# A hand-written engine order, single products between block steps, and most edge lists built inside the first batch

## The chip, the cores and the metric

The kernel runs on one core of a Trainium2 chip. The metric is the device time of one execution in microseconds (us). The kernel before takes 2917.2 us, the median of 3 runs (2911.98 to 2935.88).

## What is computed

A graph attention layer over 16 batches of 1024 nodes with 512 features and 8 heads of 64, all in float32, then a residual sum and a layer norm without weights.

```python
q = (x @ Wq + bq).reshape(b, n, H, HD)
k = (x @ Wk + bk).reshape(b, n, H, HD)
v = (x @ Wv + bv).reshape(b, n, H, HD)
scores = jnp.einsum('bqhd,bkhd->bhqk', q, k) / jnp.sqrt(jnp.float32(HD))
scores = scores + (1.0 - adj)[None, None, :, :] * -1000000000.0
attn = jax.nn.softmax(scores, axis=-1)
out = jnp.einsum('bhqk,bkhd->bqhd', attn, v).reshape(b, n, d)
return out @ Wo + bo
...
x = _layernorm(x + _L0_gnn_ref(x, adj, ...), axis=-1)
```

The adjacency matrix is the same for all 16 batches. It is sparse and uneven: entry (i, j) is 1 with a probability that falls as one over the square root of i times j, so the first rows have many neighbours and the last ones few.

## The kernel before

Scores are worked out only where the adjacency is 1. The nodes are cut into 8 tiles of 128 queries. `edges(t)` turns the rows of tile `t` into a list of edges: `MAX8` rounds find the key numbers (10 rounds for tile 0, two for each of the others), small matrix products spread them so that one edge stands on one partition, and the results are `key_row` and `query_row` (which rows to fetch) and `sums` (a 128 by 128 matrix of zeros and ones for each block, which adds the edges of a query). A block is 128 edges. `BLOCKS = (11, 6, 4, 4, 3, 3, 3, 3)` gives the blocks of each tile, 37 for one batch and 592 in all.

**The front of a batch.** For each of its 8 tiles of x: four transposes on TensorE (`transpose_x`), and three projections of four products each (`project`, 128x512 outputs): q and k leave PSUM by VectorE, v by ScalarE. q goes to the DRAM array `q_rows`, k and v to `kv_rows`, both held twice, for even and odd batches. `norm` squares q and k on ScalarE and reduces the squares on VectorE, for a guard at the end. After the last tile one small product gives the mean of v (`pm`), which is row 1024 of `kv_rows`; the gathers of a batch need that row.

**A block `n`.** GpSimd issues two indirect DMAs (`gather`): `kvg` fetches 128 rows of 1024 numbers, `qg` 128 rows of 512. `scores` multiplies q and k and reduces over each head on VectorE, then ScalarE takes the exponential; `weigh` multiplies v with it on VectorE (two instructions of 256 columns); `add_up` adds the edges on TensorE into the tile's `sum` (two products of 264 and 256 columns). After a tile's last block, `normalise` divides (VectorE) and `transpose_o` turns the result (TensorE, out by ScalarE).

**Finishing a tile.** `finish` makes the output projection `po` (four products), adds x, takes the statistics on VectorE, raises to the power -0.5 on GpSimd, scales on VectorE, and stores.

Buffers around the change: 8 `kvg` (also used by `edges`), 8 `qg`, 4 `y`, 6 `oT`, 4 PSUM banks with the tag `fill` for everything but `sum`, and 2 x 2 banks for `sum`.

**What sets the order.** The program is written as a loop over blocks: in step `n` it gathers block n + 6, scores n + 2, weighs n + 1, adds up n, and then does one piece of the next batch's front (a whole projection of four products) or, when none is left, one whole `finish`. All 8 `edges` come ahead of that loop, each followed by one tile of the front of batch 0. But this is not the order in which the engines run it: a scheduler in the framework takes the program as a priority list and reorders each engine's instructions by its own estimate of when each is ready. Within an engine the order is then fixed, and an instruction that waits holds up all behind it.

Of the kernel before, what the change touches and what calls it, by code (L numbers as in the profile page):

```python
# [24 lines left out]
KEYCODE = 2000.0  # L25
# [101 lines left out]
def kernel(  # L127
# [57 lines left out]
    with ExitStack() as main:  # L185
# [16 lines left out]
        code = one.tile([P, N], F32, name="code")  # L202
        nc.gpsimd.iota(code, pattern=[[-1, N]], base=int(KEYCODE), channel_multiplier=0, allow_small_or_imprecise_dtypes=True)

        place = one.tile([P, max(BLOCKS) * P], F32, name="place")
        nc.gpsimd.iota(place, pattern=[[1, max(BLOCKS) * P]], base=0, channel_multiplier=0, allow_small_or_imprecise_dtypes=True)
        placed = one.tile([P, max(BLOCKS)], F32, name="placed")
        nc.gpsimd.iota(placed, pattern=[[P, max(BLOCKS)]], base=0, channel_multiplier=1, allow_small_or_imprecise_dtypes=True)
# [4 lines left out]
        nc.vector.tensor_scalar(before, place[:, 0:P], query[:, 0:1], None, op0=OP.is_gt)  # L213
# [27 lines left out]
        def bias_setup():  # L241
# [7 lines left out]
            bvb = work.tile([P, NPAIR, P], F32, tag="y", name="bvb", bufs=4)  # L249
# [7 lines left out]

        def edges(t):
            nb, J = BLOCKS[t], DEGREE[t]
            a = work.tile([P, N], F32, tag="kvg", name=f"a_{t}", bufs=8)  # L260
            nc.sync.dma_start(a, adj[ds(t * P, P), :])
            v = work.tile([P, N], F32, tag="kvg", name=f"codes_{t}", bufs=8)
            nc.gpsimd.tensor_tensor(v, a, code, op=OP.mult)
            st = small.tile([P, 4], F32, name="est")
            deg, end, lim, lone = (st[:, i:i + 1] for i in range(4))
            kl = small.tile([P, J + 2], F32, tag=f"kl{J}", name=f"kl_{t}", bufs=2)

            j = work.tile([P, N], F32, tag="kvg", name=f"j_{t}", bufs=8)
            nc.scalar.activation(j, a, AF.Copy, accum_out=deg)
# [9 lines left out]
            nc.vector.tensor_scalar(lone, kl[:, 0:1], 0.0, KEYCODE - N, op0=OP.is_le, op1=OP.mult)  # L279
            nc.vector.tensor_tensor(kl[:, 0:1], kl[:, 0:1], lone, op=OP.add)  # L280
            nc.vector.tensor_scalar(deg, deg, 1.0, None, op0=OP.max)
            po = fill_psum(f"poff_{t}")
            nc.tensor.matmul(po[:, 0:1], before, deg, start=True, stop=True)
            nc.vector.tensor_copy(kl[:, J:J + 1], po[:, 0:1])
# [5 lines left out]
            )  # L290

            ge = work.tile([P, max(BLOCKS) * P], F32, tag="ge", name=f"ge_{t}", bufs=1)
            of = work.tile([P, max(BLOCKS) * P], F32, tag="of", name=f"of_{t}", bufs=1)
# [4 lines left out]
            for i0 in range(0, nb, step):  # L298
# [4 lines left out]
                for i in range(n):  # L303
                    nc.tensor.matmul(g[:, i, :], of[:, ts(i0 + i, P)], kl, start=True, stop=True)
# [211 lines left out]
        for n in range(AHEAD):  # L516
            gather(n)
# [91 lines left out]
```

## Time and profile before

| | |
|---|---|
| median of 3 runs | 2917.2 us |
| profiled execution | 2934.78 us, span 2933.0 us |
| TensorE (PE) | busy 2578.4 us, 88%, at a mean granted clock of 0.951 |
| VectorE (DVE) | busy 2013.0 us, 69% |
| GpSimd (POOL) | busy 1488.4 us, 51% |
| ScalarE (ACT) | busy 488.1 us, 17% |
| DMA | 678.04 MB, 231 GB/s over the span |

The profile is of one execution. In it, L348 is line 348 of the kernel printed above; PEld is TensorE's weight load, which overlaps PE. Each float32 matrix product of 512 columns appears as two records, so that a projection of four products is "x8". In a timeline row the columns are the start, the duration (both us), the engine, the line, the operation, output<-input and the count; in brackets stands the idle time of that engine just before, and what ended it.

### The profile page before, as it was taken

What the parts mean: (1) busy time and instruction counts of PE and PEld (TensorE: products, weight loads), DVE (VectorE), ACT (ScalarE), POOL (GpSimd) and SP (SyncE); (2) the same over time, 40 slices, a digit from 0 to 9 for tenths busy, and PEclk for the clock granted to TensorE, in tenths of its full rate; (3) what the DMA queues carried; (4) which work ended last, traced back from release to release, by engine and by line L of the source; (5) the groups of instructions that cost most, each with busy time, mean ns of one, the idle gap of its engine ahead of it and who ended that gap; (6) DMA issues with size and microseconds to landing.
All of it is one profiled execution on the core that took longest, in us unless ns stands there. A gap on an engine that the chain in (4) does not pass through costs nothing.

```text
span 2933.0 us, 27152 instructions
## 1 busy us (share of the span) xinstructions
PE 2578.4 (88%) x7659; PEld 1377.0 (47%) x7659; DVE 2013.0 (69%) x4375; ACT 488.1 (17%) x1300; POOL 1488.4 (51%) x1462
## 2 busy tenths in 40 slices
PE   2889889998989989899889988989898989989977
PEld 1445444544445444444444444444444444445443
DVE  6657756767676676766667676666756767676687
ACT  2312111111111111111111111111111111111110
POOL 3035544636455464654546455464644636455474
PEclk8999999999999999999999999999999999999988
DMA  4258776767767676776777767677766767767685
GB/s 147 79 210 279 229 243 220 264 226 247 237 225 254 235 240 233 235 250 225 250 231 255 236 214 254 227 242 240 246 230 222 257 229 244 243 225 261 209 285 168
DMA packets 228682, 678.04 MB, mean 231 GB/s; under 512 B 29454, under 2 KB 29466, under 8 KB 228524
## 3 DMA queue, kind: packets, MB, share of 16 engines
q0 software_dynamic: 132608, 465.64, 48.8%
q1 hardware_dynamic: 93344, 205.60, 20.0%
q10 hardware_dynamic: 2572, 4.99, 0.5%
q8 instruction: 63, 1.03, 0.1%
q14 instruction: 95, 0.78, 0.1%
HBM read 541.86 MB, written 134.25 MB: 231 GB/s over the span
## 4 chain that ended last, share of the span: by engine, by line
DMA 27%; DVE 25%; issue 21%; POOL 15%; PE 12%; ACT 1%; POOLq 0%; DVEq 0%; SPq 0%; ACTq 0%
DMA kvg<-kv_rows,key_row 22%; POOL qg L451 8%; DVE s L460 5%; DVE pv L468 5%; DVE qg L458 4%; POOL kvg L446 4%; PE po L424 3%; POOL rstd L433 2%; DVE kv L370 2%; DVE nrm L356 2%; DVE stats L429 2%; PE pq L348 2%; PE pv L348 2%; DVE y L426 2%; PE pk L348 2%
## 5 line engine op out<-in xcount | busy, mean ns | idle before, releaser
L446 POOL DMA_INDIRECT kvg<-kv_rows,key_row x592 | 599.0, 1012 | 907.7 <-DVE pv L468 800.5
L458 DVE TENSOR_TENSOR qg<-qg,kvg 128x512 f32<-128x512 f32 x592 | 407.6, 693 | 545.3 <-DMA kvg<-kv_rows,key_row 540.7
L451 POOL DMA_INDIRECT qg<-q_rows,query_row x592 | 615.7, 1040 | 259.6 <-issue 105.7
L348 PE MATMUL pv<-wv,xT 128*128 128x512 f32 x1024 | 481.1, 614 | 42.8 <-DVE q L363 42.8
L424 PE MATMUL po<-wo,oT 128*128 128x512 f32 x1024 | 505.0, 639 | 2.8 <-ACT oT L504 2.0
L348 PE MATMUL pq<-wq,xT 128*128 128x512 f32 x1024 | 473.1, 605 | 34.9 <-ACT xT L341 34.9
L468 DVE TENSOR_TENSOR pv<-kvg,pv 128x256 f32<-128x256 f32 x1184 | 487.7, 436 | 0.0
L348 PE MATMUL pk<-wk,xT 128*128 128x512 f32 x1024 | 460.8, 593 | 2.0 <-DVE kv L370 2.0
L460 DVE TENSOR_REDUCE s<-qg 128x8 f32<-128x512 f32 x592 | 400.3, 676 | 0.0
L481 PE MATMUL sum<-pv,sums 128*128 128x264 f32 x1184 | 371.6, 396 | 13.8 <-DVE pv L468 9.9
L482 PE MATMUL sum<-pv,sums 128*128 128x256 f32 x1184 | 363.2, 389 | 4.7 <-DVE pv L468 4.4
L424 PEld LDWEIGHTS po<-wo,oT 128*128 128x128 f32 x1024 | 206.1, 208 | 252.5 <-issue 233.0
L348 PEld LDWEIGHTS pv<-wv,xT 128*128 128x128 f32 x1024 | 199.3, 197 | 255.1 <-issue 197.7
L481 PEld LDWEIGHTS sum<-pv,sums 128*128 128x128 f32 x1184 | 218.5, 195 | 202.1 <-issue 171.9
L348 PEld LDWEIGHTS pq<-wq,xT 128*128 128x128 f32 x1024 | 193.8, 193 | 241.4 <-issue 187.9
L348 PEld LDWEIGHTS pk<-wk,xT 128*128 128x128 f32 x1024 | 185.8, 190 | 187.3 <-issue 184.1
L482 PEld LDWEIGHTS sum<-pv,sums 128*128 128x128 f32 x1184 | 229.9, 195 | 49.0 <-DVE pv L468 8.0
L356 DVE TENSOR_REDUCE nrm<-sq 128x8 f32<-128x512 f32 x256 | 174.6, 682 | 77.5 <-ACT sq L355 77.5
L355 ACT ACTIVATE sq<-q 128x512 f32<-128x512 f32 x128 | 80.6, 630 | 876.3 <-DVE q L363 755.7
L463 ACT ACTIVATE pv<-s 128x8 f32<-128x8 f32 x592 | 118.4, 203 | 546.7 <-PE sum L482 266.4
L416 POOL TENSOR_TENSOR y<-y,bo_bc 128x512 f32<-128x512 f32 x128 | 166.1, 1304 | 60.1 <-DMA y<-in_x_dram 50.3
L434 DVE TENSOR_SCALAR y<-y,mv,rstd 128x512 f32<-128x512 f32 x128 | 73.9, 577 | 162.6 <-POOL rstd L433 162.6
(96 smaller groups left out, 1551.4 us busy)
## 6 DMA issues: line engine op xcount, KB each, us to landing
kv_rows<-kv SPq DMA_DIRECT2D x128, 512.0 KB
x<-in_x_dram SPq DMA_DIRECT2D x128, 256.0 KB
y<-in_x_dram SPq DMA_DIRECT2D x128, 256.0 KB
q_rows<-q SPq DMA_DIRECT2D x128, 256.0 KB
out_dram<-y SPq DMA_DIRECT2D x128, 256.0 KB
qg<-q_rows,query_row POOLq DMA_INDIRECT x592, 5.0
kvg<-kv_rows,key_row POOLq DMA_INDIRECT x592, 5.4
a<-in_adj_dram SPq DMA_DIRECT2D x8, 512.0 KB
```

What stands on the lines that cost most here:

```text
L348: nc.tensor.matmul(p, XT[b, t][:, ts(c, P)], W[name][:, c, :], start=(c == 0), stop=(c == NPAIR - 1))
L356: nc.vector.tensor_reduce(NRM[b][:, i, t, :], sq.rearrange("p (h d) -> p h d", d=HD), axis=AX.X, op=OP.add)
L416: nc.gpsimd.tensor_tensor(y, y, bo_bc, op=OP.add)
L424: nc.tensor.matmul(p, o[:, ts(c, P)], W["o"][:, c, :], start=(c == 0), stop=(c == NPAIR - 1))
L446: nc.gpsimd.indirect_dma_start(out=KG[n], out_offset=None, in_=kv_rows[b % 2], in_offset=bass.IndirectOffsetOnAxis(ap=key_row[:, g:g + 1], ...
L451: nc.gpsimd.indirect_dma_start(out=QG[n], out_offset=None, in_=q_rows[b % 2], in_offset=bass.IndirectOffsetOnAxis(ap=query_row[:, g:g + 1] ...
L458: nc.vector.tensor_tensor(m, m, KG[n][:, 0:D], op=OP.mult)
L460: nc.vector.tensor_reduce(s, m.rearrange("p (h d) -> p h d", d=HD), axis=AX.X, op=OP.add)
L463: nc.scalar.activation(PV[n][:, HD2:HD2 + HEADS], s, AF.Exp)
L468: nc.vector.tensor_tensor(pv[:, ds(i * (HD2 + HEADS), HD2)].rearrange("p (h d) -> p h d", d=HD), v[:, ds(D + i * HD2, HD2)].rearrange("p ( ...
L481: nc.tensor.matmul(SUM[b, t][:, 0, 0:HD2 + HEADS], m, pv[:, 0:HD2 + HEADS], **kw)
L482: nc.tensor.matmul(SUM[b, t][:, 1, 0:HD2], m, pv[:, HD2 + HEADS:], **kw)
```

## The change

1. The loop over blocks stands inside `tc.manual_schedule()`: each engine runs its instructions in the order in which the program writes them. What is written before the loop is still ordered by the scheduler.
2. In that loop an operation that needs a result of step `n` from another engine is put into a later step by `later(k, fn)`: a projection's exit from PSUM comes one step after its last product, the square one step later, the reduction one more; the output's statistics follow the same rule.
3. Projections are no longer whole pieces. `product` hands out single products with a cost (`PRODUCT = 0.86`, four transposes `TRANSPOSE = 0.44`), and each step spends a fixed `share` of a batch's total cost: `per_batch / 37`.
4. `edges` became a generator of five or six pieces. Tiles 0 and 1 are built before the loop, tiles 2 to 7 inside batch 0, one piece a step, from the steps in `EDGES_FROM`.
5. Gathers run 8 blocks ahead (6 before), q ahead of k and v. The gathers of a new batch are held until the step in which that batch's mean has been stored (`set_up`).
6. `weigh` is one instruction of 512 columns; the head sums stand at the end of `pv` and not in its middle, so the two adding products have 256 and 264 columns.
7. The scale of the layer norm goes from VectorE to ScalarE (`activation` with a bias and a scale per row); for the bias GpSimd makes two more operations of 128x1 per tile. The add of x and the bias waits two steps after its load. There are 7 `y`, 7 `oT`, 7 `qg`, 2 `q`, 4 `xT`, and `edges` has two buffers of its own.

```diff
+AHEAD = 8
+EDGES_FROM = (0, 0, 1, 5, 9, 12, 15, 18)
+PRODUCT = 0.86
+TRANSPOSE = 0.44
...
+        def later(k, fn):
+            if now[0] is None:
+                fn()
+            else:
+                plan.setdefault(now[0] + k, []).append(fn)
...
+        def product(name, lhs, w, out):
+
+            def unit(c):
+                if c == 0:
+                    PS[name] = fill_psum(name)
+                p = PS[name]
+                nc.tensor.matmul(p, lhs()[:, ts(c, P)], w[:, c, :], start=(c == 0), stop=(c == NPAIR - 1))
+                if c == NPAIR - 1:
+                    del PS[name]
+                    later(1, lambda: out(p))
+
+            return [(PRODUCT, lambda c=c: unit(c)) for c in range(NPAIR)]
...
+                def root():
+                    nc.gpsimd.tensor_tensor(rstd[:, 0:1], rstd[:, 0:1], neg_half, op=OP.pow)
+                    nc.gpsimd.tensor_tensor(rstd[:, 1:2], rstd[:, 0:1], mv[:, 0:1], op=OP.mult)
+                    nc.gpsimd.tensor_tensor(rstd[:, 1:2], rstd[:, 1:2], neg_one, op=OP.mult)
+
+                def norm_out():
+                    nc.scalar.activation(y, y, AF.Identity, bias=rstd[:, 1:2], scale=rstd[:, 0:1])
+                    nc.sync.dma_start(out_ap[b, ds(t * P, P), :], y)
+                    del Y[b, t]
+
+                later(1, root)
+                later(3, norm_out)
...
         def weigh(n):
             v, pv = KG.pop(n), PV[n]
-            for i in range(2):
-                nc.vector.tensor_tensor(
-                    pv[:, ds(i * (HD2 + HEADS), HD2)].rearrange("p (h d) -> p h d", d=HD),
...
+            nc.vector.tensor_tensor(
+                pv[:, 0:D].rearrange("p (h d) -> p h d", d=HD),
+                v[:, D:].rearrange("p (h d) -> p h d", d=HD),
+                pv[:, D:, None].to_broadcast([P, HEADS, HD]), op=OP.mult,
+            )
...
+        per_batch = NT * (4 * NPAIR * PRODUCT + 2 * TRANSPOSE)
+        share = per_batch / NB
+        prep = {EDGES_FROM[t]: edges(t) for t in range(2, NT)}
+        preps = []
+        with tc.manual_schedule():
...
+            while n < total or plan or done or finishing:
+                now[0] = n
+                if n < total and blocks[n][1:] == (0, 0):
+                    b = blocks[n][0]
+                    if b + 1 < B:
+                        fronts = [u for t in range(NT) for u in front(b + 1, t)]
+                while gathered < min(n + AHEAD + 1, total) and blocks[gathered][0] in set_up:
+                    gather(gathered)
+                    gathered += 1
+                if n + 1 < total:
+                    weigh(n + 1)
+                if n + 2 < total:
+                    scores(n + 2)
+                for fn in plan.pop(n, ()):
+                    fn()
+                if n + 2 < total:
+                    exponentials(n + 2)
+                if n < total:
+                    add_up(n)
+                for bb, tt in done[:2]:
+                    if (bb, tt) not in Y:
+                        load_y(bb, tt)
+                credit += share
+                while credit > 0:
+                    if not fronts and not finishing and done and n > loaded.get(done[0], n):
+                        finishing = finish(*done.pop(0))
+                    units = finishing or fronts
+                    if not units:
+                        break
+                    cost, fn = units.pop(0)
+                    fn()
+                    credit -= cost
+                credit = min(credit, share)
+                if n in prep:
+                    preps.append(prep.pop(n))
+                preps = [g for g in preps if next(g, True) is None]
+                n += 1
```

Three places show how the instructions move. In the names, `pv_83` is the weighed block 83, `qg` and `kvg` its gathered rows, and in `po_1_0` or `y_1_0` the numbers are batch and tile.

VectorE in batch 2 (blocks 74 to 110), before:

```order
L458 TENSOR_TENSOR qg_87_3194<-qg_87_3194,kvg_87_3192 128x512
L458 TENSOR_TENSOR qg_88_3218<-qg_88_3218,kvg_88_3216 128x512
L468 TENSOR_TENSOR pv_82_3177<-kvg_82_3062,pv_82_3177 128x256 x2
L460 TENSOR_REDUCE s_85_3253<-qg_85_3140 128x8
L458 TENSOR_TENSOR qg_89_3250<-qg_89_3250,kvg_89_3248 128x512
L363 SCALAR_TENSOR_TENSOR q_3_1_3132<-pq_3_1_3127,bq_bc_104 128x512
L458 TENSOR_TENSOR qg_90_3271<-qg_90_3271,kvg_90_3269 128x512
L356 TENSOR_REDUCE nrm_3_3023<-sq_3_1_0_3135 128x8
L468 TENSOR_TENSOR pv_83_3199<-kvg_83_3094,pv_83_3199 128x256 x2
```

and VectorE there now:

```order
L520 TENSOR_TENSOR pv_83_3126<-kvg_83_2958,pv_83_3126 128x512
L509 TENSOR_TENSOR qg_84_2983<-qg_84_2983,kvg_84_2985 128x512
L511 TENSOR_REDUCE s_84_3141<-qg_84_2983 128x8
L401 TENSOR_TENSOR kv_3_2_3145<-pk_3_2_3110,bk_bc_103 128x512
L520 TENSOR_TENSOR pv_84_3147<-kvg_84_2985,pv_84_3147 128x512
L509 TENSOR_TENSOR qg_85_3016<-qg_85_3016,kvg_85_3018 128x512
L511 TENSOR_REDUCE s_85_3160<-qg_85_3016 128x8
L386 TENSOR_REDUCE nrm_3_2996<-sq_3_2_0_3143 128x8
```

Before, the product with q and k of block 90 stands ahead of the weighing of block 83, so a block's `kvg` buffer is held over seven further blocks, and the exit of the projection `q_3_1` stands behind products that need the gathers of blocks 88 and 89. Now each block is weighed one step after its scores, and a step's exits follow its one weigh and its one score.

TensorE at the mean of batch 2 (`pm_2`), in batch 1, before:

```order
L348 MATMUL pv_2_7_2639<-wv_67,xT_2_7_2527 128x512 x4
L481 MATMUL sum_1_4_2674<-pv_62_2610,sums_110 128x264
L482 MATMUL sum_1_4_2674<-pv_62_2610,sums_110 128x256
L481 MATMUL sum_1_4_2674<-pv_63_2633,sums_110 128x264
L482 MATMUL sum_1_4_2674<-pv_63_2633,sums_110 128x256
L386 MATMUL pm_2_2647<-vsum_2_2141,mean_92 1x512
L424 MATMUL po_1_0_2677<-wo_69,oT_1_0_2295 128x512 x4
```

and TensorE there now:

```order
L374 MATMUL pv_2_7_2541<-wv_67,xT_2_7_2424 128x512 x3
L553 MATMUL poT_1_3_2578<-ident_58,o_1_3_2556 128x128 x4
L532 MATMUL sum_1_4_2563<-pv_63_2534,sums_108 128x256
L533 MATMUL sum_1_4_2563<-pv_63_2534,sums_108 128x264
L356 MATMUL pxT_3_1_2591<-ident_58,x_3_1_2322 128x128 x4
L374 MATMUL po_0_6_2596<-wo_69,oT_0_6_1881 128x512 x3
L532 MATMUL sum_1_4_2563<-pv_64_2561,sums_108 128x256
L533 MATMUL sum_1_4_2563<-pv_64_2561,sums_108 128x264
L374 MATMUL po_0_6_2596<-wo_69,oT_0_6_1881 128x512
L374 MATMUL po_0_7_2623<-wo_69,oT_0_7_1966 128x512 x3
L422 MATMUL pm_2_2635<-vsum_2_2093,mean_92 1x512
```

Before, only two blocks' additions stand between the last product of v and the product that needs the sum of v. Now seven products of the output projection, eight transposes and two blocks stand there, and the output products of a tile are split by the additions.

GpSimd at the same place, before:

```order
L446 DMA kvg_76_2899<-kv_rows_0_115,key_row_111 128x1024
L416 TENSOR_TENSOR y_1_4_2654<-y_1_4_2654,bo_bc_72 128x512
L451 DMA qg_79_2972<-q_rows_0_117,query_row_112 128x512
L446 DMA kvg_77_2915<-kv_rows_0_115,key_row_111 128x1024
L433 TENSOR_TENSOR rstd_2750<-rstd_2750,neg_half_88 128x1
L451 DMA qg_80_2988<-q_rows_0_117,query_row_112 128x512
```

and GpSimd there now:

```order
L495 DMA qg_74_2698<-q_rows_0_115,query_row_110 128x512
L500 DMA kvg_74_2700<-kv_rows_0_113,key_row_109 128x1024
L495 DMA qg_75_2702<-q_rows_0_115,query_row_110 128x512
L500 DMA kvg_75_2704<-kv_rows_0_113,key_row_109 128x1024
L455 TENSOR_TENSOR y_1_1_2655<-y_1_1_2655,bo_bc_72 128x512
L471 TENSOR_TENSOR rstd_2685<-rstd_2685,neg_half_88 128x1
L472 TENSOR_TENSOR rstd_2685<-rstd_2685,mv_2682 128x1
L473 TENSOR_TENSOR rstd_2685<-rstd_2685,neg_one_90 128x1
L495 DMA qg_76_2733<-q_rows_0_115,query_row_110 128x512
L500 DMA kvg_76_2735<-kv_rows_0_113,key_row_109 128x1024
```

Before, the q gathers ran up to three blocks ahead of the k and v gathers. Now both of a block stand together, and while tiles are being finished, an add of 128x512 and three operations of 128x1 stand between the gathers of one block and the next.

More of the change, by code (lines that the diff above doesn't have):

```diff
@@ L449, in gather @@
             )
[L450 to L454 removed]
+        S = {}
         def scores(n):
```

321 lines of the change are left out of this document (152 added, 169 removed).

## The prediction

> **What bounds the kernel now.** I read the page of the profile first, for the busy shares.
>
> ```profile
> PE 2578.4 (88%) x7659; PEld 1377.0 (47%) x7659; DVE 2013.0 (69%) x4375; ACT 488.1 (17%) x1300; POOL 1488.4 (51%) x1462
> PEclk8999999999999999999999999999999999999988
> ```
>
> TensorE is the fullest engine, yet 355 us of the span are idle on it, and its granted clock is a little under full. Next I asked who waits for whom, for TensorE and for its suppliers.
>
> ```profile
> POOL kvg L446 <- DVE pv L468: 800.5, 322, 7.8
> DVE qg L458 <- DMA kvg<-kv_rows,key_row: 540.7, 361, 4.7
> PE poT L502 <- DVE o L491: 97.1, 50, 6.6
> PE pm L386 <- DVE vsum L383: 81.6, 16, 6.4
> PE pv L348 <- DVE q L363: 42.8, 22, 3.0
> ```
>
> The first two form a ring: GpSimd cannot gather because VectorE has not yet weighed the block in the buffer, and VectorE stands still for the gather. Behind that stand-still wait the operations that TensorE needs: `o`, `vsum`, the exit of q. So TensorE's main waits are those of VectorE's order, not of VectorE's load.
>
> Then the timeline of one batch, for what TensorE's work costs when nothing holds it.
>
> ```profile
> 1002.82 0.61 PE L481 MATMUL sum<-pv,sums 128*128 128x264 f32 x2
> 1003.69 3.60 PE L348 MATMUL pv<-wv,xT 128*128 128x512 f32 x8
> 1007.13 0.61 PE L481 MATMUL sum<-pv,sums 128*128 128x264 f32 x2
> 1014.28 1.87 PE L386 MATMUL pm<-vsum,mean 128*1 128x512 f32 x2 [5.24 <-DVE vsum L383]
> 1016.08 4.72 PE L424 MATMUL po<-wo,oT 128*128 128x512 f32 x8
> 1020.63 0.60 PE L502 MATMUL poT<-ident,o 128*128 128x128 f32 x4
> 1021.07 3.60 PE L424 MATMUL po<-wo,oT 128*128 128x512 f32 x8
> ```
>
> From start to start: a block's two additions 0.87 us (1002.82 to 1003.69), a projection 3.44 (1003.69 to 1007.13), four transposes 0.44 (1020.63 to 1021.07). After the wait of 5.24 us the next projection took 4.72 and not 3.60. Where TensorE was never idle, the clock was full, as this stretch shows (columns: stretch, length, busy PE, PEld, DVE, ACT, POOL, clock, DMA share, GB/s):
>
> ```profile
> 240.00:280.00 40.00, 40.00 (x124) 21.72 (x123) 26.13 (x55) 8.28 (x23) 18.42 (x20) 1.00 0.79 257
> ```
>
> A batch therefore needs 32 projections x 3.44 + 37 blocks x 0.87 + 16 sets of transposes x 0.44 + 0.9 for the mean = 110.1 + 32.2 + 7.0 + 0.9 = 150.2 us of TensorE. What it takes now follows from the first and last of the 16 means:
>
> ```profile
> 185.58 1.02 PE L386 MATMUL pm<-vsum,mean 128*1 128x512 f32 x2 [1.40 <-DVE vsum L383]
> 2767.76 1.86 PE L386 MATMUL pm<-vsum,mean 128*1 128x512 f32 x2 [5.57 <-DVE vsum L383]
> ```
>
> (2767.8 - 185.6) / 15 = 172.1 us. So the span is 185.6 of start, 15 x 172.1, and 165.2 of end, and the gap between 172.1 and 150.2 is what an order can win.
>
> **The period of a batch.** Does the new order supply TensorE? First the gathers.
>
> ```profile
> 2765.60 0.94 POOL L446 DMA_INDIRECT kvg<-kv_rows,key_row  x1 [0.39 <-DVE pv L468]
> 2772.29 0.69 DVE L458 TENSOR_TENSOR qg<-qg,kvg 128x512 f32<-128x512 f32 x1 [2.15 <-DMA kvg<-kv_rows,key_row]
> 2773.54 0.94 POOL L446 DMA_INDIRECT kvg<-kv_rows,key_row  x1 [1.92 <-DMA kv_rows<-mean]
> 2845.38 0.93 POOL L446 DMA_INDIRECT kvg<-kv_rows,key_row  x1 [0.30 <-issue]
> 2847.88 1.02 POOL L446 DMA_INDIRECT kvg<-kv_rows,key_row  x1 [0.30 <-DVE mv L430]
> ```
>
> A gather's rows are in use 6.7 us after its issue (2765.60 to 2772.29). Now a gather of block n + 8 is issued in step n, behind the weighing of block n, and its scores stand in step n + 6: about 25 us at 4.2 us a step. The buffers are no longer held over seven blocks, so the ring opens. At a batch's turn the gathers wait for the mean; by the order of GpSimd shown above they come one step late, which 25 us cover.
>
> Next VectorE. Its three operations of a block:
>
> ```profile
> L458 DVE TENSOR_TENSOR qg<-qg,kvg 128x512 f32<-128x512 f32 x592 | 407.6, 693 | 545.3 <-DMA kvg<-kv_rows,key_row 540.7
> L468 DVE TENSOR_TENSOR pv<-kvg,pv 128x256 f32<-128x256 f32 x1184 | 487.7, 436 | 0.0
> L460 DVE TENSOR_REDUCE s<-qg 128x8 f32<-128x512 f32 x592 | 400.3, 676 | 0.0
> ```
>
> The one weighing of 512 columns does not stand in the trace; between the product of 512 (0.69) and two halves (0.87) I take 0.70, as it has the shape of the former. So weigh and scores are 2.07 us of a 4.2 us step. All of VectorE's 2013 us, without any saving, would be 76% of a span of 2660: it has room. An exit that waits for TensorE holds up the next step's weigh, but that weigh is needed only a whole step later. The scaling of the norm leaves VectorE for ScalarE, which is 17% busy; I price both at nothing while ScalarE's exponentials stay ahead of the weighing.
>
> GpSimd is the tight one. A pair of gathers takes 2.50 us (2845.38 to 2847.88). A finished tile adds:
>
> ```profile
> L433 POOL TENSOR_TENSOR rstd<-rstd,neg_half x128: 547/587/1213, 319.1 to 2925.8; 128x1 f32<-128x1 f32 x128
> L416 POOL TENSOR_TENSOR y<-y,bo_bc 128x512 f32<-128x512 f32 x128 | 166.1, 1304 | 60.1 <-DMA y<-in_x_dram 50.3
> ```
>
> that is 1.3 + 0.6 (the middle number, a median in ns), and two multiplications of 128x1 that the trace does not show. At least they cost nearly nothing, at most the power's 0.6 each; I take 0.35, the middle, and 0.3 for gaps: 2.9 us a tile. A step on TensorE is 0.87 + the share (32 x 0.86 x 4 + 16 x 0.44 = 117.1 us by the constants, over 37: 3.17) + 0.19 for the transposes of `o` = 4.23 us. Fronts use 8 x (3 x 3.44 + 0.44) = 86.1 us, 27 steps; then 8 tiles are finished in 8.7 steps. In these, a GpSimd step is 2.50 + 2.9 / 1.09 = 5.2 us against 4.23: 8 us behind at the end, about the two steps that the program leaves between the power on GpSimd and the scaling on ScalarE. What it costs lies between 0 and 8 us a batch; I take 3.4 with everything else that may jolt, clock dips included. Lastly, the share counts the transposes of `o`, which are done outside it, so 117.1 - 113.6 = 3.5 us a batch stay unused: one step without products, which VectorE sets at some 3.3 us (2.07 and a finished tile's exit and statistics, an estimate) against 0.9 on TensorE: 2.4. The period: 150.2 + 2.4 + 3.4 = 156.
>
> **The start.** Rows of the first list and of the fronts:
>
> ```profile
> 38.80 2.98 POOL L263 TENSOR_TENSOR codes<-a,code 128x1024 f32<-128x1024 f32 x1
> 39.51 3.35 DVE L275 SCALAR_TENSOR_TENSOR codes<-codes,kl 128x1024 f32<-128x1024 f32 x1
> L275 DVE SCALAR_TENSOR_TENSOR codes<-codes,kl x16: 1261/1282/3384, 13.4 to 144.9; 128x1024 f32<-128x1024 f32 x16
> L273 DVE MAX8 kl<-codes 128x8 f32<-128x1024 f32 x24 | 28.9, 1218 | 7.9 <-POOL codes L263 7.8
> 57.03 4.99 PE L304 MATMUL pe<-kl,of 128*128 128x82 f32 x22 [23.57 <-DVE kl L273]
> 65.89 3.70 PE L348 MATMUL pq<-wq,xT 128*128 128x512 f32 x8 [0.68 <-ACT xT L341]
> 180.58 3.60 PE L348 MATMUL pv<-wv,xT 128*128 128x512 f32 x8
> ```
>
> The chain to 57.03 loses what the scheduler put between tile 0's rounds for tiles 1 and 2 (four MAX8 and two maskings, 7.2) and two maskings drawn out to 3.4 beside GpSimd (4.2): 45.7. Tile 0's rest was 8.9, now 7.1 as x is transposed earlier: the first projection at 52.8. The fronts ran from 65.9 to 184.2, 118.3 us, of which 86.1 are products; the other 32.2 are seven lists of 4.6. One is left: 52.8 + 86.1 + 4.6 + 1.4 (the wait at 185.58) = 145 to the first mean, 41 earlier.
>
> Two things are paid back. TensorE now has the first addition ahead of its next products, and cannot fill the time until gathered rows are there: from mean to k and v gather 5.8 us (2767.76 to 2773.54), 6.7 to use, 2.3 for scores, exponential and weigh, less 1.6 of its own work: 13 us. And six lists move into batch 0: two MAX8, one masking and some 3 us of small operations each (an estimate), 40 us of VectorE in 22 steps that have 1 us free each, and two steps of slack: 40 - 22 - 6 = 12 us, between 0 (all hidden) and 20 (no slack used). Their loads go through SP ahead of that step's stores, and their multiplications through GpSimd, 3.0 us as at 38.80, ahead of the next step's gathers: the 25 us of lead cover both, and without it each would cost its 3 us.
>
> **The end.** In the last batch there are no fronts.
>
> ```profile
> 2892.90 1.00 POOL L451 DMA_INDIRECT qg<-q_rows,query_row  x1 [0.17 <-issue]
> ```
>
> 37 pairs took from 2773.54 to 2893.9, 120 us, set by GpSimd. The new multiplications add 16 x 0.7 = 11; the 39 us from the last gather to the end shrink by about as much, since scores no longer queue. I leave 165.
>
> **The sum.** 145 + 13 + 12 + 15 x 156 + 165 = 2675 us of span and about as much for the execution. The profiled one took 2934.78, the median 2917.2: a factor of 0.994, so 2660.
>
> **The rivals.** Less than 1%, 29 us, cannot be told from no change.
>
> *TensorE fully fed.* No jolts, no loss in batch 0: 145 + 13 + 15 x 152.6 + 165 = 2612, so 2596; without the empty step too, 2560. For it speaks the stretch with 40.00 busy of 40; against it, that nothing in this trace lasts longer than that. 0.13.
>
> *GpSimd falls behind while tiles are finished.* The late power holds the scaling on ScalarE, behind it stand the exponentials, the weighing and the additions. The two rows at 38.80 and 39.51 show GpSimd and VectorE drawing each other out. If each of a tile's four operations waits out a VectorE product of 0.69, a GpSimd step grows by 2.5 to 7.7, 30 us behind per batch less 8 of slack: a period of 174 and 2930. With half of that, 164: 145 + 25 + 2460 + 165 = 2795, so 2780. Against it: the power's median is 40 ns over its shortest, so most met no lock. 0.15, at 2780. The Trainium skill has the rule in SBUF — State Buffer, section "SBUF: two separate sides": a GpSimd operation that reads SBUF and a VectorE operation with two SBUF inputs exclude one another for a whole instruction. By that rule, taken at every operation, the time would be the 2930 above; the drawn-out masking agrees with it, the power's median does not show it as a regular cost.
>
> *The order wins nothing inside a batch.* VectorE goes on waiting for gathers, with the DMA engines at 0.79 in the stretch above already; the period stays at 172: 145 + 25 + 2582 + 165 = 2917, so 2899. It needs gathers to take four times the 6.7 us. 0.09.
>
> *Slower: the four PSUM banks.* The exit of a projection now stands behind the next step's weigh and scores, 2.07 us, and the next product but two needs that bank. In the table of waits that is `PE pv <- DVE q`: 42.8 us, 22 times, 1.9 each. If each of 32 projections waits 0.73, the period is 152.6 + 23.4 = 176: 145 + 25 + 2640 + 165 = 2975, so 2957. It decides from 0.71 us a projection on. Against it, three other projections' or transposes' work lies between exit and reuse. 0.09.
>
> **Numbers.** My forecast has 0.54, with a range of its own of 2610 to 2720 (periods of 153 to 160). Faster: 0.54 + 0.13 + 0.15 = 0.82; within 1%: 0.09; slower: 0.09. The range from 2560 to 2850 leaves out the last two rivals, and reaches to a period of 168.
>
> **What would show it.** Right: 15 intervals between means of some 156 us, the first one longer; a clock near 1.00; the waits of GpSimd for `pv` and of VectorE for `kvg` nearly gone; first mean near 145. Wrong: TensorE waiting at a projection for an exit (banks), ScalarE at the scaling for `rstd` (GpSimd), or VectorE for gathers as before.

## The result, and the profile after

The changed kernel takes 2706.42 us (median of 4 runs, 2704.45 to 2707.88) where the kernel before takes 2921.54 (4 runs, 2911.98 to 2935.88): a ratio of 0.926, 95% interval 0.922 to 0.930. The profiled execution took 2707.88 us with a span of 2706.1. The forecast was 2660.

The page of the changed kernel, busy shares, clock, and the projections of v with the wait ahead of them:

```profile
PE 2507.0 (93%) x7659; PEld 1376.4 (51%) x7659; DVE 2004.2 (74%) x3655; ACT 614.3 (23%) x1428; POOL 1531.2 (57%) x1717
PEclk8988999999999999999999999999999999999878
L374 PE MATMUL pv<-wv,xT 128*128 128x512 f32 x1024 | 488.2, 606 | 0.3 <-DVE q L394 0.3
```

TensorE's idle time fell from 355 to 199 us. Its mean granted clock rose from 0.951 to 0.966, and its stages differ, as four windows from stage to stage show (columns as in the prediction; the clock is the third number from the end):

```profile
0.00:144.39 144.39, 105.64 (x293) 53.55 (x293) 66.43 (x110) 30.05 (x49) 8.61 (x16) 0.94 0.30 106
144.39:321.50 177.11, 144.00 (x449) 80.12 (x450) 134.72 (x277) 50.59 (x106) 96.15 (x81) 0.89 0.70 238
321.50:2516.68 2195.18, 2130.24 (x6555) 1168.72 (x6554) 1672.89 (x3011) 504.93 (x1198) 1305.99 (x1478) 0.99 0.81 265
2516.68:2706.10 189.42, 127.14 (x365) 74.00 (x364) 130.17 (x258) 28.76 (x75) 120.47 (x143) 0.82 0.60 199
```

The third, the 14 full periods, is nearest to full clock, at 0.99 (0.96 in the kernel before). The changed kernel's table of waits (total us, times, longest):

```profile
POOL qg L495 <- DVE s L511: 558.4, 309, 3.6
DVE y L462 <- POOL y L455: 105.8, 23, 7.1
PE poT L553 <- DVE o L544: 105.1, 33, 10.6
ACT y L476 <- POOL rstd L473: 56.4, 29, 7.4
DVE qg L509 <- DMA kvg<-kv_rows,key_row: 11.6, 5, 9.7
```

VectorE's wait for gathered rows fell from 540.7 to 11.6 us, and GpSimd's wait for `pv`, 800.5 before, is not in the table any more. The wait that was 97.1 of TensorE for `o` is still there, with another cause ahead of it: VectorE now waits for GpSimd's add of x and bias (`y L455`). The first three means and the last, from the timeline, give the stages:

```profile
144.39 1.02 PE L422 MATMUL pm<-vsum,mean 128*1 128x512 f32 x2 [1.40 <-DVE vsum L418]
...
321.50 1.02 PE L422 MATMUL pm<-vsum,mean 128*1 128x512 f32 x2
...
475.10 1.02 PE L422 MATMUL pm<-vsum,mean 128*1 128x512 f32 x2
...
2516.68 1.02 PE L422 MATMUL pm<-vsum,mean 128*1 128x512 f32 x2
```

144.4 to the first mean, 177.1 for the first interval, (2516.7 - 321.5) / 14 = 156.8 for the others, 189.4 from the last mean to the end. Two windows of one batch (columns as in the prediction) show where TensorE still stands still:

```profile
440.00:480.00 40.00, 40.00 (x123) 21.33 (x122) 32.54 (x64) 8.60 (x22) 20.09 (x22) 1.00 0.80 269
480.00:520.00 40.00, 35.93 (x114) 19.70 (x113) 32.09 (x62) 8.46 (x18) 32.74 (x43) 1.00 0.75 241
```

The second is where tiles are finished: GpSimd is 33 of 40 us busy, and its 0.3 us of issue between gathers is not counted in that. In the timeline of that window, rows of GpSimd and VectorE:

```profile
493.27 2.39 DVE L520 TENSOR_TENSOR pv<-kvg,pv 128x512 f32<-128x512 f32 x1
...
493.82 1.27 POOL L455 TENSOR_TENSOR y<-y,bo_bc 128x512 f32<-128x512 f32 x1
...
495.05 1.04 POOL L471 TENSOR_TENSOR rstd<-rstd,neg_half 128x1 f32<-128x1 f32 x1
...
513.15 1.27 POOL L455 TENSOR_TENSOR y<-y,bo_bc 128x512 f32<-128x512 f32 x1
...
514.46 0.69 DVE L462 TENSOR_TENSOR y<-po,y 128x512 f32<-128x512 f32 x1 [5.36 <-POOL y L455]
...
519.12 0.68 PE L553 MATMUL poT<-ident,o 128*128 128x128 f32 x4 [2.60 <-DVE o L544]
```

VectorE waits 5.36 us for the add, with weigh, scores and `o` queued behind that wait, and then TensorE waits 2.60 for `o`. The weighing that has GpSimd's add beside it here takes 2.39 us; the median is 0.68.

### The profile page after: what moved, and what is told of

Its sections match the earlier page's. It is cut to its first block, busy times and chain, and to the rows that moved or that the text cites. A ratio compares the mean times of both kernels' runs of the same rounds, so it can differ in the third digit from the quotient of the medians.

```text
span 2706.1 us, 26468 instructions
## 1 busy us (share of the span) xinstructions
PE 2507.0 (93%) x7659; PEld 1376.4 (51%) x7659; DVE 2004.2 (74%) x3655; ACT 614.3 (23%) x1428; POOL 1531.2 (57%) x1717
## 4 chain that ended last, share of the span: by engine, by line
PE 71%; DVE 13%; POOL 7%; issue 6%; DMA 2%; ACT 1%; SPq 0%; POOLq 0%; DVEq 0%; ACTq 0%
PE pv L374 16%; PE pk L374 14%; PE pq L374 14%; PE po L374 8%; PE sum L533 7%; PE sum L532 7%; POOL kvg L500 3%; DVE pv L520 3%; DVE qg L509 2%; PE pxT L356 2%; DVE y L462 2%; DVE stats L465 2%; POOL qg L495 2%; PE poT L553 2%; DVE s L511 2%
## 5 line engine op out<-in xcount | busy, mean ns | idle before, releaser
L495 POOL DMA_INDIRECT qg<-q_rows,query_row x592 | 589.1, 995 | 781.0 <-DVE s L511 558.4
L520 DVE TENSOR_TENSOR pv<-kvg,pv 128x512 f32<-128x512 f32 x592 | 431.9, 730 | 265.5 <-ACT pv L516 236.4
L374 PE MATMUL pk<-wk,xT 128*128 128x512 f32 x1024 | 479.3, 597 | 4.5 <-ACT kv L407 4.5
L374 PE MATMUL pq<-wq,xT 128*128 128x512 f32 x1024 | 482.0, 597 | 0.0
L374 PE MATMUL po<-wo,oT 128*128 128x512 f32 x1024 | 469.6, 599 | 0.0
L509 DVE TENSOR_TENSOR qg<-qg,kvg 128x512 f32<-128x512 f32 x592 | 427.0, 721 | 11.6 <-DMA kvg<-kv_rows,key_row 11.6
L374 PEld LDWEIGHTS pk<-wk,xT 128*128 128x128 f32 x1024 | 196.1, 192 | 208.7 <-issue 195.1
L374 PEld LDWEIGHTS po<-wo,oT 128*128 128x128 f32 x1024 | 196.9, 193 | 190.3 <-issue 178.6
L374 PEld LDWEIGHTS pq<-wq,xT 128*128 128x128 f32 x1024 | 187.8, 192 | 144.2 <-issue 136.1
L462 DVE TENSOR_TENSOR y<-po,y 128x512 f32<-128x512 f32 x128 | 87.9, 687 | 152.5 <-POOL y L455 105.8
L455 POOL TENSOR_TENSOR y<-y,bo_bc 128x512 f32<-128x512 f32 x128 | 164.7, 1287 | 57.2 <-DMA y<-in_x_dram 50.9
L553 PE MATMUL poT<-ident,o 128*128 128x128 f32 x512 | 86.4, 293 | 109.5 <-DVE o L544 105.1
```

What stands on the lines that cost most here:

```text
L374: nc.tensor.matmul(p, lhs()[:, ts(c, P)], w[:, c, :], start=(c == 0), stop=(c == NPAIR - 1))
L455: later(2, lambda: nc.gpsimd.tensor_tensor(Y[b, t], Y[b, t], bo_bc, op=OP.add))
L462: nc.vector.tensor_tensor(y, p, y, op=OP.add)
L495: nc.gpsimd.indirect_dma_start(out=QG[n], out_offset=None, in_=q_rows[b % 2], in_offset=bass.IndirectOffsetOnAxis(ap=query_row[:, g:g + 1] ...
L509: nc.vector.tensor_tensor(m, m, KG[n][:, 0:D], op=OP.mult)
L520: nc.vector.tensor_tensor(pv[:, 0:D].rearrange("p (h d) -> p h d", d=HD), v[:, D:].rearrange("p (h d) -> p h d", d=HD), pv[:, D:, None].to ...
```

## The experiments

Theory at the start: VectorE's order carries the gain, and GpSimd, behind while tiles are finished, keeps the rest. The rivals are that the program's other parts carry the gain, and that loads or GpSimd's sum of work keep the rest. The stages of every run in us, from its rows of the means (to the first mean; first interval; mean of the other 14 intervals, the period; from the last mean to the end), its median, and its ratio to the kernel before in the same comparison:

| run | first mean | 1st interval | period | end | median us | ratio, 95% |
|---|---|---|---|---|---|---|
| changed kernel | 144.4 | 177.1 | 156.8 | 189.4 | 2706.4 | 0.922-0.930 |
| e_sched | 153.1 | 148.7 | 181.2 | 164.3 | 2999.5 | 1.017-1.026 |
| e_whole | 144.2 | 167.7 | 157.4 | 191.3 | 2709.1 | 0.919-0.927 |
| e_lists | 171.3 | 140.3 | 156.7 | 186.3 | 2692.3 | 0.913-0.921 |
| e_yload | 144.1 | 177.5 | 151.1 | 173.4 | 2613.2 | 0.887-0.893 |
| e_ylate | 144.6 | 177.8 | 156.4 | 189.9 | 2701.0 | 0.917-0.924 |
| e_yalldve | 144.2 | 176.4 | 151.1 | 172.3 | 2610.6 | 0.887-0.894 |
| e_yscale | 143.3 | 176.4 | 158.3 | 169.3 | 2707.6 | 0.920-0.927 |
| e_yadj | 142.8 | 171.3 | 151.1 | 172.7 | 2605.9 | 0.886-0.892 |
| e_ahead6 | 144.3 | 174.3 | 152.9 | 185.9 | 2653.5 | 0.901-0.906 |
| e_best | 144.4 | 162.3 | 156.4 | 166.2 | 2662.0 | 0.902-0.908 |
| e_vec6 | 144.2 | 161.7 | 151.6 | 162.8 | 2588.9 | 0.878-0.882 |
| e_vec8 | 143.5 | 170.3 | 151.6 | 159.0 | 2596.8 | 0.882-0.885 |

### Which part carries the gain

**The order given back to the scheduler.** (e_sched)

```diff
-        with tc.manual_schedule():
+        with ExitStack():
```

> The program is unchanged, but each engine's order is again the scheduler's and not the program's own. Theory (the gain is the order of VectorE, one weighing and one block's scores a step): the scheduler again takes several blocks' products of q and k ahead of the weighing, VectorE's wait for gathered rows goes from 12 us back above 200, the period from 157 to 165-172, the time to 2830-2920 us. Rival (the gain lies in what the program states in any order: gathers eight blocks ahead, exits a step later, single products): 2680-2735 us, with VectorE's wait for gathers below 60.

2999.5 us: the rest of the change, without the order by hand, is 1.7 to 2.6% slower than the kernel before. Two rows of its waits, and from its timeline the second and the last mean:

```profile
DVE qg L509 <- DMA kvg<-kv_rows,key_row: 698.2, 349, 6.0
POOL kvg L500 <- DVE pv L520: 588.8, 197, 7.1
```

```profile
301.82 1.02 PE L422 MATMUL pm<-vsum,mean 128*1 128x512 f32 x2
...
2839.04 1.02 PE L422 MATMUL pm<-vsum,mean 128*1 128x512 f32 x2
```

The ring of the kernel before is back, and the period of 181.2 is longer than the 175.6 that the kernel before has over the same 14 intervals. The rival is out, and the theory's size was too small: the order is worth some 290 us here, not 125 to 215. This run gives all engines back to the scheduler, so it shows the worth of the hand-written order as a whole; that VectorE's part of it carries the gain is read from the waits, and no run changes VectorE's order alone.

**The products of a projection together again.** (e_whole)

```diff
-            return [(PRODUCT, lambda c=c: unit(c)) for c in range(NPAIR)]
+            def all_units():
+                for c in range(NPAIR):
+                    unit(c)
+            return [(NPAIR * PRODUCT, all_units)]
```

> The four products of a projection stand together again; all else as in the changed kernel. Theory (order of VectorE carries the gain, TensorE's spreading little, since the weighing is a step ahead of its additions): a step without a projection takes TensorE 0.9 us and the next one 4.3 or more, and a period loses 0 to 2 us: 2700-2740 us. Rival (single products are what keeps TensorE fed): additions wait for their weighing in most steps without a projection, some 1.2 us each in 5 to 10 steps a batch, 2790 us or more.

2709.1 us, an interval that overlaps the changed kernel's: spreading single products wins nothing that can be measured. (The first interval is 9 us shorter, the period 0.6 longer.)

**All edge lists ahead of the loop.** (e_lists)

```diff
-            if t < 2:
+            if t < NT:
                 for _ in edges(t):
-        prep = {EDGES_FROM[t]: edges(t) for t in range(2, NT)}
+        prep = {EDGES_FROM[t]: edges(t) for t in range(NT, NT)}
```

> All eight edge lists are built ahead of the loop instead of two. By the prediction's terms a list ahead of the loop costs 4.6 us and six in the first batch cost 12: first mean at 144 + 28 = 172, first interval 177 - 12 = 165, together +16: 2722 us. By what the changed trace shows (first interval 177.1, the others 156.8, of which 13 for the ramp) only 7 are to be won back: +21, 2727 us. Rival (lists ahead of the loop lie beside TensorE's projections and cost it little): first mean below 155, the time 2690-2710 us.

2692.3 us, 14 faster where 16 to 21 slower was expected, and not by the rival: the first mean came at 171.3 as expected. What failed is the first interval, 140.3 us and not 165. The first two means in its timeline:

```profile
171.30 1.02 PE L422 MATMUL pm<-vsum,mean 128*1 128x512 f32 x2 [1.40 <-DVE vsum L418]
...
311.63 1.02 PE L422 MATMUL pm<-vsum,mean 128*1 128x512 f32 x2
```

Six lists inside the first batch thus cost 36.8 us, and 26.9 ahead of it: moving them is a loss of 10 to 14 us.

### What keeps the rest

**x loaded and added early.** (e_yload) `ready` gets a tile when its sum is normalised.

```diff
-                for bb, tt in done[:2]:
-                    if (bb, tt) not in Y:
-                        load_y(bb, tt)
+                if ready and len(Y) < 6:
+                    load_y(*ready.pop(0))
```

> x is loaded again, and the bias added to it on GpSimd, as soon as a tile's sum is normalised (up to six tiles waiting), not two tiles at a time while the tiles are finished. Theory (what is left of TensorE's idle time is GpSimd behind in the finishing steps: VectorE waits for the added x and bias, o stands behind that): VectorE's wait for GpSimd's y falls from 106 us below 20, TensorE's for o from 105 below 60, the period from 156.8 to 153-154, the end from 189 to 176-182 us: 2640-2660 us. Rival (GpSimd's gathers and powers alone keep it behind; the wait moves to the power): 2690-2706 us with ScalarE's wait for rstd above 60. Rival 2 (loads earlier collide with gathers on the DMA engines): slower than 2706.

2613.2 us, more than the theory asked for: period 151.1, next to the 150.2 that the prediction counted as TensorE's work, end 16 us shorter. VectorE's wait for the add is nearly gone, as two rows of its waits show:

```profile
DVE y L462 <- POOL y L455: 10.7, 5, 4.6
PE poT L553 <- DVE o L544: 9.1, 7, 3.5
```

**Early load, late add.** (e_ylate) The load as above; the add is put in the order where the changed kernel has it.

```diff
+        def add_y(b, t):
             loaded[b, t] = now[0]
-            nc.sync.dma_start(Y[b, t], x[b, ds(t * P, P), :])
             later(2, lambda: nc.gpsimd.tensor_tensor(Y[b, t], Y[b, t], bo_bc, op=OP.add))
...
+                if ready and len(Y) < 6:
+                    load_y(*ready.pop(0))
                 for bb, tt in done[:2]:
-                    if (bb, tt) not in Y:
-                        load_y(bb, tt)
+                    if (bb, tt) in Y and (bb, tt) not in loaded:
+                        add_y(bb, tt)
```

> x is loaded again at a tile's normalising, as in the run with the early load and add (2613 us), but GpSimd's add of the bias stands where the changed kernel has it, two tiles at a time while tiles are finished. Theory (GpSimd's work bunched in the finishing steps was the cause): nothing is won over the changed kernel, 2690-2706 us, VectorE's wait for GpSimd's y again near 100. Rival (the cause was the load's landing, for which GpSimd waited 50.9 us with gathers and powers queued behind): 2613-2640 us, period 151-153.

2701.0 us. The load's landing is out; it is where the add stands on GpSimd.

**The late add on VectorE.** (e_yalldve)

```diff
-            later(2, lambda: nc.gpsimd.tensor_tensor(Y[b, t], Y[b, t], bo_bc, op=OP.add))
+            later(2, lambda: nc.vector.tensor_tensor(Y[b, t], Y[b, t], bo_bc, op=OP.add))
```

> The changed kernel, with the add of x and bias on VectorE (0.69) in place of GpSimd (1.29), at its old, late place. Theory (GpSimd's bunched work): a finishing step on GpSimd falls from about 4.9 to 3.7 us, below TensorE's 4.2, the period goes to 151-154, 2620-2660 us. Rival (the load's landing): VectorE now waits for the load itself, in its own queue, 2690-2730 us.

2610.6 us, 9 below the expected range, with 128 more operations on VectorE. Its busy time rose by 24 us only, though the adds are 128 x 0.68 = 87. The line of the weighing in the changed kernel, and then in this one (shortest/median/longest in ns), shows why:

```profile
L520 DVE TENSOR_TENSOR pv<-kvg,pv x592: 675/682/2394, 155.7 to 2678.5; 128x512 f32<-128x512 f32 x198
```

```profile
L520 DVE TENSOR_TENSOR pv<-kvg,pv x592: 674/683/758, 155.5 to 2579.9; 128x512 f32<-128x512 f32 x198
```

Without GpSimd's adds no weighing is drawn out. That saves VectorE 28 us at the weighing and 22 at the product of q and k, most of the difference. So the late add takes GpSimd's own time, and VectorE's while the two exclude each other. But the exclusion alone is not what it cost. The run with the early load and add has more of it, as the weighing's rows on the pages of the changed kernel and of that run show (busy us, mean ns of one):

```profile
L520 DVE TENSOR_TENSOR pv<-kvg,pv 128x512 f32<-128x512 f32 x592 | 431.9, 730 | 265.5 <-ACT pv L516 236.4
```

```profile
L520 DVE TENSOR_TENSOR pv<-kvg,pv 128x512 f32<-128x512 f32 x592 | 460.5, 778 | 285.4 <-ACT pv L516 221.9
```

Its weighings and products together are drawn out by 60 us, against 50 in the changed kernel, and it is 93 us faster, with the same period as this run. What counts is whether the delay reaches TensorE, which it does in the steps that finish tiles; how much of it there is GpSimd's own time and how much VectorE's, these runs do not part.

**The norm's scaling back on VectorE** (e_yscale), on top of early load and add:

```diff
-                    nc.gpsimd.tensor_tensor(rstd[:, 1:2], rstd[:, 0:1], mv[:, 0:1], op=OP.mult)
-                    nc.gpsimd.tensor_tensor(rstd[:, 1:2], rstd[:, 1:2], neg_one, op=OP.mult)
...
-                    nc.scalar.activation(y, y, AF.Identity, bias=rstd[:, 1:2], scale=rstd[:, 0:1])
+                    nc.vector.tensor_scalar(y, y, mv[:, 0:1], rstd, op0=OP.subtract, op1=OP.mult)
```

> Early load and add (2613 us), and the norm's scaling back on VectorE, without GpSimd's two multiplications of 128x1. Theory (with GpSimd no longer behind, TensorE sets the period at 151 and neither place matters): 2605-2625 us. Rival (VectorE at the scaling waits for the power, as 0.4 to 0.8 us a tile in the kernel before, and more while GpSimd is late): 2640 us or more. Rival 2 (the two multiplications still hold GpSimd in the last batch): 2590-2600 us.

2707.6 us, 94 over the run with the scaling on ScalarE, and not by the rival: VectorE waits for the power 2.7 us in all. VectorE's and GpSimd's timelines in a finishing phase:

```profile
486.75 2.33 DVE L518 TENSOR_TENSOR pv<-kvg,pv 128x512 f32<-128x512 f32 x1
...
490.32 0.54 DVE L474 TENSOR_SCALAR y<-y,mv,rstd 128x512 f32<-128x512 f32 x1
...
492.50 2.32 DVE L518 TENSOR_TENSOR pv<-kvg,pv 128x512 f32<-128x512 f32 x1
```

```profile
487.25 1.27 POOL L455 TENSOR_TENSOR y<-y,bo_bc 128x512 f32<-128x512 f32 x1
488.47 1.03 POOL L471 TENSOR_TENSOR rstd<-rstd,neg_half 128x1 f32<-128x1 f32 x1
...
490.68 1.04 POOL L493 DMA_INDIRECT qg<-q_rows,query_row  x1 [1.19 <-DVE s L509]
...
493.00 1.27 POOL L455 TENSOR_TENSOR y<-y,bo_bc 128x512 f32<-128x512 f32 x1
```

The two engines hold each other up. GpSimd's gather waits for VectorE's scores, whose buffer it needs; after the gathers come the add and the power, and the add meets the next weighing, which ends 1.6 us late, and the scores behind it too. Such a step takes 5.75 us (486.75 to 492.50) against TensorE's 4.2. Not every step has an add that meets a weighing: the six steps from the weighing at 477.43 to that at 507.49 take 5.0 us in the mean, and three of their weighings are drawn out. That 0.54 us more on VectorE is what closes this ring is how I read it; the run shows the ring and the loss.

**Gathers six blocks ahead** (e_ahead6), as in the kernel before (there with 8 buffers for q's rows, here 7):

```diff
-AHEAD = 8
+AHEAD = 6
```

> The changed kernel with gathers issued six blocks ahead instead of eight; the buffers (7 for q's rows, 8 for k's and v's) as they are. Theory (with a lead of eight the buffers let GpSimd be only one step ahead of VectorE, for whose scores it waits 558 us; six leave it three steps, 8 us more, as much as it falls behind while tiles are finished): VectorE's wait for GpSimd's y falls from 106 us below 40, the period from 156.8 to 151-153, the end from 189 to 165-178: 2610-2640 us. Rival (the bunched work keeps GpSimd behind whatever the lead): 2690-2706 us. Rival 2 (four steps, 17 us, no longer cover a gather): VectorE's wait for k's and v's rows from 12 to over 100 us, 2720 us or more.

2653.5 us: a lead of eight made the changed kernel 53 us slower. The time is above the expected range: the period is as expected (152.9), the end, 185.9, was not won. VectorE's wait for GpSimd's add fell from 105.8 to 46.7 us, and GpSimd's for VectorE's scores from 558.4 to 341.1. With eight ahead and 7 buffers a gather needs the scores of the step before; with six, GpSimd can run further ahead of VectorE.

### Towards a better kernel

**Adjacency tiles two steps early in the first batch** (e_yadj), on top of early load and add:

```diff
-EDGES_FROM = (0, 0, 1, 5, 9, 12, 15, 18)
+EDGES_FROM = (0, 0, 0, 3, 7, 10, 13, 16)
...
             nc.sync.dma_start(a, adj[ds(t * P, P), :])
+            yield
+            yield
```

> Early load and add (2613 us), and in the first batch each adjacency tile is loaded two steps ahead of GpSimd's multiplication by it. Theory (lists in the first batch cost what they do because GpSimd waits 39.5 us for these loads and VectorE 22.8 for GpSimd): the first interval falls from 177.5 to 158-164 us, 2594-2600 us. Rival (it is VectorE's 40 us of work on the lists): the first interval stays at 172-178, 2608-2615 us.

2605.9 us, between the two expectations. GpSimd's wait for these tiles in the first batch fell from 40.7 to 2.0 us, but the interval only by 6, to 171.3: mostly the rival. Of the lists' 37 us the waiting is the smaller part.

**All three together** (e_best: early load and add, early adjacency tiles, six ahead):

> Together: early load and add, adjacency tiles two steps early in the first batch (2606 us with these two), and gathers six blocks ahead. Theory (GpSimd and VectorE no longer wait for each other): the period stays at 151, as TensorE sets it, and the last batch, where the two set the pace, shrinks: end 173 to 150-160, 2580-2595 us. Rival (the last batch goes by GpSimd's own sum of work): 2600-2608 us.

2662.0 us, a miss: the end shrank to 166, but the period rose to 156.4. A finishing phase in its timelines of VectorE and of GpSimd:

```profile
645.48 2.29 DVE L522 TENSOR_TENSOR pv<-kvg,pv 128x512 f32<-128x512 f32 x1
```

```profile
645.94 1.27 POOL L457 TENSOR_TENSOR y<-y,bo_bc 128x512 f32<-128x512 f32 x1
647.16 1.03 POOL L473 TENSOR_TENSOR rstd<-rstd,neg_half 128x1 f32<-128x1 f32 x1
```

Again the add meets the weighing, though not in every step. Two changes that win 93 and 53 us alone win 44 together. My reading is that they change when the two engines meet; how often they meet does not show it (weighings over 0.8 us: 76 in the run before this one, 61 with the lead of six alone, 54 here). Two last runs take GpSimd's add out of it, one with a lead of six (e_vec6), one with eight (e_vec8).

```diff
-            later(2, lambda: nc.gpsimd.tensor_tensor(Y[b, t], Y[b, t], bo_bc, op=OP.add))
+            later(2, lambda: nc.vector.tensor_tensor(Y[b, t], Y[b, t], bo_bc, op=OP.add))
```

> Early load, adjacency tiles two steps early, gathers six blocks ahead as in the combined run (2662 us), and the add of x and bias on VectorE instead of GpSimd. Theory (the combined run lost because GpSimd's add fell on VectorE's weighing and the two took turns: 2.29 us for a weighing of 0.68): no weighing is longer than 0.8 us, the period falls from 156.4 to 150.5-152, the end from 166 to 158-166: 2580-2600 us. Rival (six blocks of lead is itself too short): the period stays at 155 or more, 2640-2665 us. Rival 2 (VectorE, with 0.69 more a tile, is too full): period 153-155, 2615-2640 us.

> The same with gathers eight blocks ahead, as in the changed kernel. Theory: the period at 151 as well, the end at 170-174 as in the two runs with a lead of eight and no late add: 2596-2608 us, some 10 us over the lead of six. Rival (the lead is what matters, whatever engine adds): equal to the early-load run within 5 us, and the lead of six slower by 40 or more.

2588.9 and 2596.8 us, both in the expected ranges: 0.880 and 0.883 of the kernel before, against 0.926 of the changed kernel. The period is 151.6 in both, so the lead by itself was not at fault in the combined run. The run with a lead of eight is 8 us slower as forecast, but by luck: the theory put the loss at the end (170 to 174), which measured 159.0, shorter than the 162.8 with six, and it lies in the first interval, 170.3 against 161.7. In each run one weighing and one product of the first batch were still drawn out (1.53 and 2.83 us with six, 3.18 and 2.84 with eight), each beside GpSimd's multiplication of 128x1024 for a list.

## Why the prediction was right, and where it was wrong

The chain that carried it held: VectorE's wait for gathers opened, and the run with the scheduler's order shows that it is the order by hand that opens it. Term by term, of the span of 2675 against 2706:

- **Start, 145.** Measured 144.4.
- **Ramp, 13.** TensorE was idle for 10.46 us ahead of the first addition, and the first projection took 5.12 us instead of 3.60: 12.
- **Lists in the first batch, 12, and a whole period beside them.** The first interval came out as forecast (177.1 against 13 + 12 + 156 = 181), for two errors that cancel. The lists cost 36.8 (run with all lists ahead); the bound of 20 was wrong too. And the interval holds less than a period: in that run 29 blocks' additions and under two output projections (58 and 14 records in the means' interval), where a period has 37 and 8: 8 x 0.87 + 6.25 x 3.44 = 28.5 us less. The trace of the kernel before had this already, in the row of its second mean:

```profile
310.08 1.86 PE L386 MATMUL pm<-vsum,mean 128*1 128x512 f32 x2 [6.43 <-DVE vsum L383]
```

Its first interval is 124.5 us and the other 14 are 175.6 in the mean; the prediction's 172.1 averages over both.
- **Period, 156.** Measured 156.8, of it 14: +11 us. Its parts were off. The 2.4 for a step without products is at most 0.9: the early-load run keeps that step and has 151.1 against 150.2 of work. The lag that GpSimd's late add brings, taken as 3.4 within 0 to 8, is 156.8 - 151.1 = 5.7. The window of the same 14 periods in the early-load run parts it:

```profile
321.57:2437.05 2115.48, 2104.24 (x6555) 1157.27 (x6554) 1681.67 (x3015) 504.63 (x1199) 1328.15 (x1480) 1.00 0.83 276
```

Of the 5.7 us, 3.8 are idle time of TensorE and 1.9 are longer busy time, at a granted clock of 0.99 against 1.00. So the size of the period is in part luck: one term was too large, the other too small. The sum of a step, 4.23, has a slip too: its 0.19 counts 16 sets of transposes, and the 8 of `o` make 0.095.
- **End, 165: the step that failed.** It measured 189.4, 24 of the 31 us that the span was short. The gathers were nearly right: in the timeline of the changed kernel they run from 2522.36 to 2655.57, 133 us, against 120 + 11.

```profile
2522.36 1.03 POOL L495 DMA_INDIRECT qg<-q_rows,query_row  x1 [0.61 <-issue]
...
2654.62 0.95 POOL L500 DMA_INDIRECT kvg<-kv_rows,key_row  x1 [0.30 <-issue]
...
2686.79 8.73 PE L374 MATMUL po<-wo,oT 128*128 128x512 f32 x16
```

That "the 39 us from the last gather to the end shrink by about as much" was wrong: they grew to 50.5. With a lead of eight, not six, more blocks are left when the last gather is issued; in the run with six this tail is 45.5, 5.0 less. The larger part goes with the late add and with what hangs on it: the program starts a tile's output projection only in a step after that in which its add is asked for (`n > loaded`), and so the last two projections stood together, 8.73 us of TensorE behind everything else. With the early load and add they stand apart, 3.60 and 3.70, and the tail (from 2573.6) is 36.8. The early load alone does not help: with the late add the tail is 52.9, and the two projections are together again. With the late add on VectorE they are together too (7.03), and the tail is 45.6; how much of the rest is GpSimd's and how much the start of the projections, no run parts.
- **From span to median, 0.994.** Taken from one kernel's profile and median; here it is 0.9995, which makes 15 of the 46 us.
- **Prices.** The new multiplications have a median of 0.19 us on GpSimd (taken: 0.35), the power 0.88 (taken: 0.6), the weighing 0.68 (taken: 0.70). "Both at nothing" for the scaling on ScalarE was not tested in the changed kernel itself; put back on VectorE in the early-load run, it costs 94 us.

The rivals: *TensorE fully fed* is not what the changed kernel does, but inside the periods it is what its early-load variant does. *The order wins nothing* is out with the wait for gathers, and *the PSUM banks* too: TensorE waited 0.3 us for the exit of q, before 42.8, and 4.5 for that of v. *GpSimd falls behind* was half right: it does, yet at 5.7 us a batch and not 8 or more, and through another place, VectorE's wait for the add of x and bias (105.8) rather than ScalarE's for the power (56.4). Against that rival I had held the power's median, 40 ns over its shortest. That evidence didn't carry over: the power's median is 0.88 us now, its shortest 0.55. And the trace before had a sign of the other kind, a longest weighing of 2.08 us where the median is 0.42. The rule that I had set aside, of the Trainium skill, SBUF — State Buffer, section "SBUF: two separate sides" (a GpSimd operation that reads SBUF and a VectorE operation with two SBUF inputs exclude one another), agrees with these traces: a weighing of 0.68 took up to 2.39 us beside GpSimd's add, and none took more than 0.76 in the run that only moved the adds to VectorE.

## What to carry to other kernels

When an order is written by hand, find for each pair of engines how many steps one may run ahead of the other, from the buffers and the lead together: a longer lead with the same buffers ties them closer, and cost 53 us in the changed kernel, though only 8 once the add was off GpSimd. Spread work that is bunched in one phase over the phase where its engine is idle, and look at the last stage of a kernel on its own, with what is left after its last transfer. A term that comes out right can be two errors; only a run that changes it alone tells.

## What the runs showed of the hardware

In the changed kernel 46 of VectorE's products of two SBUF tiles (29 weighings, 17 products of q and k) took more than 0.8 us, up to 2.39 instead of 0.68, and each of them ended 0.55 or 0.56 us after an add of 128x512 on GpSimd (1.27 us). The power behind such an add waits in its turn: in the row at 495.05 it took 1.04 us, where its shortest is 0.55, and it ended 0.43 us after the weighing. Reductions, with one SBUF input, were never drawn out (0.685 to 0.689 us for all 592). Moving the 128 adds onto the busier of the two engines made the kernel 96 us faster, yet the early-load run, which leaves them on GpSimd and has more drawn-out products, is as fast within 3 us. So it was not how often the two engines met that decided, but whether TensorE came to wait for it: it was idle for 65 us of the 14 periods in the changed kernel, and for 11 in the early-load run. I had expected a rare cost.
